# Message passing on one core: the sums move from VectorE's adds to ScalarE's copy and a store into two tables, and the column copies go from 40 to 52 per step

## The chip, the cores and the metric

The kernel runs on one core of a Trainium2 chip. The metric is the device time of one execution in microseconds. The engines that matter are TensorE (PE), VectorE (DVE), ScalarE (ACT), GpSimd (POOL), which issues the gathers, and SyncE (SP), which issues most other DMAs. Each engine has a queue of instructions of its own, which it works through in order.

## The reference

One layer of message passing over a graph of 12500 nodes and 212500 edges, then a residual and a layer norm. `src` and `dst` are the two ends of each edge; the edges come sorted by `dst`.

```python
msg_in = concat([x[src], x[dst], edge_attr])            # 64 + 64 + 32 columns
messages = relu(msg_in @ mW1 + mb1) @ mW2 + mb2         # 128 hidden columns, 64 out
aggregated = segment_sum(messages, dst, 12500)
upd = relu(concat([x, aggregated]) @ uW1 + ub1) @ uW2 + ub2
out = layernorm(x + upd)
```

All is float32. Since the second product is linear, the kernel sums the hidden rows (128 columns) per node and multiplies the sums by the combined weights `wc` = mW2 x uW1; the bias `mb2` comes in by the count of edges of each node.

## The kernel before, in words

**Groups and steps.** The edges are cut into G = 554 groups of 384 (three tiles of 128). The nodes that one group's edges end at lie in a window of W = 32 consecutive nodes. The main loop has a step per group `k`; the order on each engine is the order in which the code is written. Four things are in work at once:

- POOL gathers the source rows `x[src]` of group `k + 16`, one indirect DMA per tile (`gather`, L184), into a ring of 20 buffers `own_s`. A gather may start when the buffer's last user, 20 groups before, is done.
- PE transposes group `k` (`turn`, L429), multiplies group `k - 2` by the message weights (`hidden`, L453), and sums group `k - 4` (`sums`, L481 and L486). The three make one step with a wait in front and a signal behind it; there are two sets of PSUM buffers.
- ACT copies the transposed rows out of PSUM into `own_st` (L440), whose other 32 rows are edge features that SP loads every four steps (L359). SP also loads the window of projected destination rows, `by_dst`, into the moving weights `own_wm`, four steps ahead (L402).
- DVE applies the relu of `hidden` (L464, PSUM to `own_h`), adds the sums of `k - 4` into `own_agg` (L493) and its counts into row 96 of `own_xc` (L494), both at an address held in a register, and writes the one-hot rows of group `k + 6` (`onehot`, L412). The registers of four groups' addresses are loaded by a TENSOR_LOAD (`places`, L371) every fourth step.

**Copied columns.** 54 of the groups aren't gathered. Their 64-row columns are copied one by one from `own_xc`, which holds all of x transposed, into `own_st`: 40 columns per step, at addresses that come from an index tile by TENSOR_LOAD (`registers`, L576; `fetch`, L597 on DVE and L599 on ACT). DVE has `VCOLS = (12, 8)` and ACT `ACOLS = (8, 4, 4, 4)`: one load per entry, then that many copies of 64 x 4 bytes. The copies run from step 18 to step 536. SP fetches the indices of 8 steps at once (L555), and DVE turns them into addresses (L561).

**Update.** When a chunk of 512 nodes has all its sums, six stages turn it into output, one stage per step (`update`): inner (PE, L504 and L505), relu (ACT, L510), outer (PE), stats (DVE), root (ACT), scaled (DVE, then the store of the output). There are 25 chunks, and one is in work at a time. The last ten steps of the loop copy no columns and split the PE step into pieces; the sums of the last groups and the last chunk follow.

A second path, `unordered`, is there for edges whose windows don't fit; it doesn't run on this data.

Of the kernel before, what the change touches and what calls it, by code (L numbers as in the profile page):

```python
# [20 lines left out]
P = 128  # L21
N = 12500
# [15 lines left out]
NW = 2 * SB  # L38
COUNT = 96
NH = 3  # L40
# [9 lines left out]
TIMES = 4  # L50
BEGIN = 18
CHECKED = 8
VCOLS = (12, 8)
ACOLS = (8, 4, 4, 4)
# [49 lines left out]
class Own:  # L104
# [4 lines left out]
    def __init__(self, nc, ctx):  # L109
        def on(name, *shape, of=nc.sbuf_tensor):  # L110
            return ctx.enter_context(of(name, list(shape), F32)).ap()

        self.s = [on(f"own_s{i}", P, TG, D + W) for i in range(RING)]
        self.st = [on(f"own_st{i}", P, SB * GE) for i in range(BLOCKS)]
# [8 lines left out]
        self.agg = on("own_agg", P, NP)  # L123

        self.ps = [[on(f"own_ps{i}{k}", P, 512, of=nc.psum_tensor) for k in range(3)]
                   for i in range(2)]
# [3 lines left out]
def ordered(ctx: ExitStack, tc: tile.TileContext, a, own, ok):  # L130
# [14 lines left out]
    xc, agg = own.xc, own.agg  # L145
    xc_bytes = xc.bitcast(U8)

# [74 lines left out]
    def rest(n0, n1):  # L222

        nc.scalar.activation(xc[D : COUNT + 1, n0:n1],
                             ident[D : COUNT + 1, D : D + 1].to_broadcast([W + 1, n1 - n0]),
                             AF.Copy)
# [23 lines left out]
    def zeroed(k):  # L250

        n0, n1 = (NP * i // BITS for i in (k, k + 1))
        nc.vector.memset(agg[:, n0:n1], 0.0)

    halves = [(0, G // 2), (G // 2, G)]
    firsts_f = [own.ps[k][2][:, : g1 - g0] for k, (g0, g1) in enumerate(halves)]
# [22 lines left out]
    start_i = const.tile([1, G], I32, name="start_i")  # L279
    start_b = const.tile([1, G], I32, name="start_b")  # L280

    def placed():

        for f, (g0, g1) in zip(firsts_f, halves):
            nc.vector.tensor_scalar(start_f[:, g0:g1], f[0:1, :], 0.0, None, ALU.max)
        nc.vector.tensor_tensor(start_f, start_f, high, ALU.min)
        nc.vector.tensor_copy(start_i, start_f)
        nc.vector.tensor_scalar(start_b, start_f, 4.0 * H, None, ALU.mult)
# [4 lines left out]
    ux = const.tile([COUNT + 1, H], F32, name="ux")  # L293
# [3 lines left out]
    def update_weights():  # L297

        nc.vector.memset(ux, 0.0)
# [11 lines left out]
    starts, rows_at, indices, columns_by = {}, {}, {}, {}  # L311
# [4 lines left out]
    by_dst = dram.tile([NP, H], F32, name="by_dst")  # L316
    written = []

    up = None

    def combined():

        wps = ups.tile([H, CH], F32, name="u_ps").rearrange("p (n h) -> p n h", n=4)
        nc.tensor.matmul(wps[:, 0], w2t, u1s, start=True, stop=True)
        nc.tensor.matmul(wps[0:1, 1], b2, u1s, start=True, stop=True)
        nc.vector.tensor_copy(wc, wps[:, 0])
        nc.vector.tensor_copy(ux[COUNT : COUNT + 1, :], wps[0:1, 1])

    def ordered_edges():
# [10 lines left out]
        wrong = temp.tile([1, 2, G], F32, name="wrong")  # L340
# [4 lines left out]
        nc.vector.tensor_tensor(wrong[:, 1], first_f, high, ALU.is_gt)  # L345
        nc.vector.tensor_reduce(nwrong, wrong, mybir.AxisListType.XY, ALU.add)
# [8 lines left out]
    def inputs(b):  # L355
# [3 lines left out]
        efs_by[b] = nc.sync.dma_start(own.st[b % BLOCKS][D + W :, : c1 - c0], a["efT"][:, c0:c1])  # L359
        after(efs_by[b], *([hidden_by[(b - BLOCKS + 1) * SB - 1]] if b >= BLOCKS else []))  # L360

    def columns(g):
        t, c = own.st[g // SB % BLOCKS], (g % SB) * GE
        return t, c, sum(tiles_of(g))

    def places(b):

        g, n = b * SB, min(SB, G - b * SB)
        if n <= 0:
            return  # L370
        _, v = nc.values_load_multi_w_load_instructions(  # L371
            start_i[0:1, g : g + n], engines=[ET.DVE], min_val=0, max_val=N - 1,
            skip_runtime_bounds_check_because="they were clamped to the nodes on the chip",
        )
        for i in range(n):
            starts[g + i] = v[i]
# [13 lines left out]
    def window(g):  # L390
# [3 lines left out]
        if g % SB == 0:  # L394
            n = min(SB, G - g)
            _, v = nc.values_load_multi_w_load_instructions(
                start_b[0:1, g : g + n], engines=[ET.SP], min_val=0, max_val=4 * H * (N - 1),
                skip_runtime_bounds_check_because="they were clamped to the nodes on the chip",
            )
            rows_at.update(zip(range(g, g + n), v))  # L400
# [21 lines left out]

    def turn(g, ps):
# [3 lines left out]
        xt = ps[0][: D + W, :GE]  # L427
# [7 lines left out]
        def copy(step):  # L435
            t, c, n = columns(g)
            turn_by[g] = step
            r = slice(D if g in columned else 0, D + W)
            copies = [ordered_by_steps(
                after(nc.scalar.activation(t[r, c : c + n], xt[r, :n], AF.Copy), step))]  # L440
# [7 lines left out]
    def hidden(g, ps):  # L448
        t, c, n = columns(g)
        sizes = tiles_of(g)  # L450
        pre = ps[1][:, : TG * H].rearrange("p (j h) -> p j h", h=H)
# [5 lines left out]
        needs = [*copy_by[g], *columns_by.get(g, {}).values(), wm_by[g], efs_by[g // SB],  # L457
                 *(wm_loads[g] if g < NW else ())]

        def relu(step):  # L460
# [7 lines left out]
            for i in relu_by[g]:  # L468
                after(i, step, *([sums_by[g - NH]] if g >= NH else []))
            return relu_by[g]  # L470
# [3 lines left out]
    def sums(g, ps):  # L474
        h, s = own.h[g % NH], own.s[g % RING]
        sizes = tiles_of(g)
        sg = ps[2][:, : TIMES * W].rearrange("p (t w) -> p t w", w=W)
        counted = ps[2][0:1, TIMES * W :][:, :W]
        did = []
        for j, p in enumerate(sizes):  # L480
            did.append(nc.tensor.matmul(  # L481
                sg, h[:p, j, :],
                s[:p, j, D:].unsqueeze(1).to_broadcast([p, TIMES, W]),
                start=j == 0, stop=j == len(sizes) - 1))
        for j, p in enumerate(sizes):
            did.append(nc.tensor.matmul(counted, own.one[:p], s[:p, j, D:],  # L486
                                        start=j == 0, stop=j == len(sizes) - 1))

        def add(step):
            sums_by[g] = step  # L490
            at = bass.ds(starts.pop(g), W)
            count = xc[COUNT : COUNT + 1, at]
            a = after(nc.vector.tensor_tensor(agg[:, at], sg[:, 0, :], agg[:, at], ALU.add), step)  # L493
            return [a, after(nc.vector.tensor_tensor(count, counted, count, ALU.add), step)]  # L494

        return did, [*relu_by[g], *copy_by[g]], add

    def update(base, p, n):
# [3 lines left out]
        def inner():  # L502
            u_ps = ups.tile([H, CH], F32, name="u_ps")
            nc.tensor.matmul(u_ps[:, :q], wc, agg[:, rows], start=True, stop=False)  # L504
            nc.tensor.matmul(u_ps[:, :q], ux, xc[: COUNT + 1, rows], start=False, stop=True)  # L505
# [42 lines left out]
        return [inner, relu, outer, stats, root, scaled]  # L548
# [14 lines left out]
    def registers(k, *parts):  # L563
# [5 lines left out]
        for part in parts:  # L569
# [11 lines left out]
            held[part] = engine, c0, v  # L581

    def fetch(part, first=None):
# [79 lines left out]
    def step_update(g):  # L663

        nonlocal now
        if not now and waiting and waiting[0][0] <= g:
# [6 lines left out]
    users = {part: [[], []] for part in (turn, hidden, sums)}  # L673

    def step(*work):
# [3 lines left out]
        for part, g in work:  # L679
            ps, old = own.ps[g % 2], users[part][g % 2]  # L680
# [7 lines left out]
        for g in [g for part, g, *_ in parts if part is sums]:  # L688
            step_update(g)
        for part, g, _, _, follow in parts:  # L690
            users[part][g % 2] = follow(did[-1])
# [4 lines left out]
    places(0)  # L696
    weights(SB)
    inputs(0)
    for i in (0, 1):
        zeroed(i)  # L700
# [15 lines left out]
    for k in range(G):  # L716
        if k < BITS:
            bit(k)
            if k + 2 < BITS:
                zeroed(k + 2)  # L720
        if 1 < k < len(TABLE):
            projected(k)
        if k == CHECKED:
# [6 lines left out]
            up = ctx.enter_context(tc.tile_pool(name="upd", bufs=2))  # L730
        if k % SB == 2:
            inputs(k // SB + 2)
        if k % SB == 1:
            places(k // SB + 1)
        if k < G - SHORT:
            step((turn, k), *([(hidden, k - 2)] if k > 1 else []),
                 *([(sums, k - 4)] if k > 3 else []))
            made, summed = max(0, k - 1), max(0, k - 3)
# [15 lines left out]
        window(k + SB)  # L754
        for n in range(len(STREAMS)):
# [17 lines left out]
    while summed < G:  # L773
        step((sums, summed))
        summed += 1
    while now or waiting:
        step_update(G)
# [17 lines left out]
def unordered(ctx: ExitStack, tc: tile.TileContext, a, own):  # L795
# [9 lines left out]
    src_sb, dst_sb = (own.agg[:, i * (NF + 1) : (i + 1) * (NF + 1)].bitcast(I32) for i in (0, 1))  # L805
    nc.sync.dma_start(src_sb, src)
    nc.scalar.dma_start(dst_sb, dst[:, : NF + 1])
# [41 lines left out]
    dst_f, away = (own.agg[:, i * (NF + 1) : (i + 1) * (NF + 1)] for i in (2, 3))  # L849
    nc.vector.tensor_copy(dst_f, dst_sb)  # L850
    nc.vector.tensor_scalar(away, dst_f, -1.0, spare, ALU.mult, ALU.add)
# [36 lines left out]
    with tc.tile_pool(name="zef", bufs=3) as efp, tc.tile_pool(  # L888
# [16 lines left out]
        def gather(g):  # L905
            m, p = tiles(g)
            at = 4 * (NF + 1) + g % (NEAR + 2) * 2 * R * H
            s, d = (own.agg[:, at + i * R * H :][:, : R * H].rearrange("p (r h) -> p r h", h=H)
                    for i in (0, 1))
            for j in range(m):  # L910
                t = g * R + j
                for o, table, idx in ((s, by_src, src_sb), (d, by_dst, dst_sb)):
                    nc.gpsimd.indirect_dma_start(
                        out=o[:p, j, :], out_offset=None, in_=table[:, :],
                        in_offset=bass.IndirectOffsetOnAxis(ap=idx[:p, t : t + 1], axis=0),
                    )
            gathered[g] = s, d
# [138 lines left out]
def gnn_layer(ctx: ExitStack, nc, a):  # L1056
# [4 lines left out]
    with tc.manual_schedule():  # L1061
        ordered(tc, a, own, ok)
    good = nc.values_load(ok[0:1, 0:1], min_val=0, max_val=1,
                          skip_runtime_bounds_check_because="a comparison's result")
    with tc.If(good == 0):
        with tc.manual_schedule():
            unordered(tc, a, own)
# [38 lines left out]
```

## Time and profile before

| | |
|---|---|
| median of 3 executions | 1895.83 us (1894.88 to 1898.73) |
| profiled execution | 1894.96 us, of which 1893.1 us is the span of the trace |
| granted TensorE clock, mean | 0.963 |
| gathers (L184) | 1499, 1417.3 us busy |
| DVE: column copies (L597) / relu (L464) / one-hot (L412) | 894.5 / 303.1 / 135.7 us busy |
| DVE: adds of counts (L494) and of sums (L493) | 102.0 / 97.9 us busy |
| ACT: column copies (L599) / copy of turned rows (L440) | 1089.2 / 267.3 us busy |

The busy time of a line is what its instructions took on the engine. Where the rows name DVEq, ACTq or SPq, they mean the engine's queue: a TENSOR_LOAD fills registers there, FUSED_REGOPS computes an address, and neither counts as busy time of the engine, though nothing behind it is issued in that time. "a/b/c" in a row are the shortest, the median and the longest of its instructions in ns.

### The profile page before, as it was taken

The page shows a single profiled execution, that of the slowest core. Times are in us where ns is not written, and L with a number is a line of the kernel's source. Part 1 is how long each engine was busy: PE and PEld are TensorE (multiplying, and loading weights), DVE is VectorE, ACT ScalarE, POOL GpSimd, SP SyncE. Part 2 cuts the span into 40 slices and gives each one's busy share as a digit, 9 for nine tenths or more (in the row PEclk, how much of TensorE's full clock was granted, in tenths as well). Part 3 has the DMA queues.
Part 4 walks back from the last instruction along what each step waited for, and adds up shares of the span by engine and source line. Part 5 has one row for each costly group of instructions (what it writes and reads, how often), then busy time and mean ns, then how long its engine had stood idle before and what let it go on. Part 6 is the DMA issues. An engine that isn't in the chain of part 4 may idle for free. (4 is left out here: it accounts for less than half of the span.)

```text
span 1893.1 us, 60001 instructions
## 1 busy us (share of the span) xinstructions
PE 1336.2 (71%) x12323; PEld 1182.5 (62%) x12323; DVE 1475.6 (78%) x13054; ACT 1385.6 (73%) x11008; POOL 1418.0 (75%) x1506
## 2 busy tenths in 40 slices
PE   5877777757667666777677766776766757666767
PEld 4766666656556555666566665666666656656666
DVE  4468898878878788778887887878878888788763
ACT  3368888877777777777787777777777877777741
POOL 7777777777777777777777777777777777777774
PEclk9789999999999999989998999999999999999998
DMA  5542222222222222222222222222222222222221
GB/s 144 138 98 64 54 51 53 48 51 48 45 53 53 46 52 48 50 49 50 49 53 46 52 45 53 53 46 53 48 51 48 48 51 53 45 54 48 50 48 28
DMA packets 113382, 104.90 MB, mean 55 GB/s; under 512 B 51873, under 2 KB 83246, under 8 KB 113006
## 3 DMA queue, kind: packets, MB, share of 16 engines
q0 software_dynamic: 47968, 49.19, 13.6%
q1 hardware_dynamic: 64194, 51.30, 10.0%
q14 instruction: 272, 2.23, 0.4%
q8 instruction: 104, 1.70, 0.4%
q10 hardware_dynamic: 844, 0.48, 0.1%
HBM read 91.19 MB, written 9.62 MB: 53 GB/s over the span
## 5 line engine op out<-in xcount | busy, mean ns | idle before, releaser
L184 POOL DMA_INDIRECT own_s<-in_x,src_sb x1499 | 1417.3, 945 | 457.9 <-DMA own_s<-in_x,src_sb 206.3
L599 ACT ACTIVATE own_st<-own_xc 64x4 uint8 x10360 | 1089.2, 191 | 66.7 <-issue 18.6
L597 DVE COPY own_st<-own_xc 64x4 uint8 x10376 | 894.5, 191 | 171.1 <-issue 146.9
L429 PE MATMUL own_ps<-own_ident,own_s 128*96 128x128 f32 x1661 | 292.4, 287 | 512.0 <-ACT own_st L599 230.9
L440 ACT ACTIVATE own_st<-own_ps 96x384 f32<-96x384 f32 (+1 forms) x554 | 267.3, 483 | 383.0 <-PE own_ps L486 341.6
L429 PEld LDWEIGHTS own_ps<-own_ident,own_s 128*96 128x96 f32 x1661 | 166.4, 130 | 572.8 <-ACT own_st L599 311.4
L481 PE MATMUL own_ps<-own_s,own_h 128*128 128x128 f32 x3322 | 483.7, 284 | 1.9 <-DVE own_h L464 1.3
L453 PE MATMUL own_ps<-own_wm,own_st 128*128 128x128 f32 x3322 | 479.9, 283 | 0.0
L481 PEld LDWEIGHTS own_ps<-own_s,own_h 128*128 128x128 f32 x3322 | 436.0, 200 | 3.8 <-DVE own_h L464 2.4
L464 DVE TENSOR_SCALAR own_h<-own_ps 128x384 f32<-128x384 f32 x553 | 303.1, 548 | 167.4 <-PE own_ps L486 152.3
L453 PEld LDWEIGHTS own_ps<-own_wm,own_st 128*128 128x128 f32 x3322 | 431.7, 198 | 1.4 <-issue 0.5
L486 PE MATMUL own_ps<-own_s,own_one 128*1 128x32 f32 x3322 | 190.0, 194 | 0.0
L486 PEld LDWEIGHTS own_ps<-own_s,own_one 128*1 128x1 f32 x3322 | 114.5, 84 | 70.1 <-issue 7.2
L412 DVE TENSOR_TENSOR own_s<-iota,dlc 128x96 f32<-128x96 f32 x554 | 135.7, 246 | 0.8
L494 DVE TENSOR_TENSOR own_xc<-own_ps,own_xc 1x32 f32 x554 | 102.0, 184 | 28.8 <-PE u_ps L505 11.0
L493 DVE TENSOR_TENSOR own_agg<-own_ps,own_agg 128x32 f32 x554 | 97.9, 177 | 18.1 <-PE own_ps L486 10.3
L383 PE MATMUL u_ps<-w1b,own_xc 65*128 65x128 f32 x196 | 33.9, 325 | 28.6 <-DMA own_xc<-in_xT 12.6
L383 PEld LDWEIGHTS u_ps<-w1b,own_xc 65*128 65x128 f32 x196 | 28.7, 225 | 31.3 <-issue 20.3
L517 PE MATMUL u_ps<-same,own_xc 65*128 65x64 f32 (+1 forms) x196 | 39.5, 284 | 0.5 <-ACT u L510 0.5
L386 ACT ACTIVATE t<-u_ps 128x512 f32<-128x512 f32 (+1 forms) x25 | 14.7, 587 | 33.4 <-DMA by_dst<-t 16.7
L519 PE MATMUL u_ps<-u,u 128*128 128x64 f32 (+1 forms) x196 | 38.3, 277 | 0.0
L517 PEld LDWEIGHTS u_ps<-same,own_xc 65*128 65x128 f32 (+1 forms) x196 | 29.9, 192 | 2.4 <-ACT u L510 0.8
(60 smaller groups left out, 262.1 us busy)
## 6 DMA issues: line engine op xcount, KB each, us to landing
own_st<-in_efT SPq DMA_DIRECT2D x138, 192.0 KB
own_s<-in_x,src_sb POOLq DMA_INDIRECT x1499
own_wm<-by_dst SPq DMA_DIRECT2D x554, 16.0 KB
by_dst<-t SPq DMA_DIRECT2D x24, 256.0 KB
out<-o SPq DMA_DIRECT2D x24, 128.0 KB
own_xc<-in_xT SPq DMA_DIRECT2D x12, 179.2 KB
index<-in_src_copied SPq DMA_DIRECT2D x64, 1.2 KB
dlc_i<-in_dst_cols SPq DMA_DIRECT2D x1, 807.0 KB
```

What stands on the lines that cost most here:

```text
L184: nc.gpsimd.indirect_dma_start(out=s[:p, j, :D], out_offset=None, in_=x[:, :], in_offset=bass.IndirectOffsetOnAxis(ap=src_sb[:p, g * TG + ...
L412: places_by[g] = nc.vector.tensor_tensor(own.s[g % RING][:, :, D:], iota.unsqueeze(1).to_broadcast([P, TG, W]), dlc[:, g * TG : (g + 1) * ...
L429: nc.tensor.transpose(xt[:, j * P : j * P + p], sides[g] if g in sides and j == TG - 1 else s[:p, j, :], ident[:p, :p])
L440: after(nc.scalar.activation(t[r, c : c + n], xt[r, :n], AF.Copy), step))]
L453: nc.tensor.matmul(pre[:p, j, :], t[:, c + j * P : c + j * P + p], wm[g % NW], start=True, stop=True)
L464: relu_by[g] = [nc.vector.tensor_scalar(h, pre, 0.0, None, ALU.max)]
L481: did.append(nc.tensor.matmul(sg, h[:p, j, :], s[:p, j, D:].unsqueeze(1).to_broadcast([p, TIMES, W]), start=j == 0, stop=j == len(sizes) - 1))
L486: did.append(nc.tensor.matmul(counted, own.one[:p], s[:p, j, D:], start=j == 0, stop=j == len(sizes) - 1))
L493: a = after(nc.vector.tensor_tensor(agg[:, at], sg[:, 0, :], agg[:, at], ALU.add), step)
L494: return [a, after(nc.vector.tensor_tensor(count, counted, count, ALU.add), step)]
L597: by[engine] = nc.vector.tensor_copy(o, x_at)
L599: by[engine] = nc.scalar.activation(o, x_at, AF.Copy)
```

## The change

**Sums and counts.** PE's `sums` now has the one-hot rows (32 columns) on the stationary side and the hidden rows on the moving side, so that a group's sums are 32 rows of 128, with the count as column 129. They go into rows 64 to 95 of the PSUM buffer that holds the transposed rows of the same step, beside them. ACT's copy of the turned rows takes 513 columns instead of 384 and moves both. SP then stores 64 rows of 129 floats (the 32 nodes of the window, and 32 rows of zeros behind them) into a table in DRAM, at the address of the group's first node; even and odd groups go to two tables, `by_node0` and `by_node1`. DVE's adds, their address computations, `own_agg` and the loads of `places` are gone; SP's register loads hold two addresses per group. `hidden` is 3 steps behind `turn` instead of 2, and `sums` 6 instead of 4; the PSUM buffer of `hidden` is one of its own, `own_pre`.

**Update.** A chunk starts two steps later and has twelve stages: a load of its rows from both tables (two DMAs), one step of waiting, the transposed counts (PE), their copy (ACT), the transposed sums, added over both tables in PSUM (PE), their copy (DVE, 128 x 512), and then the six stages of before, with three products in `inner`.

**Columns.** `VCOLS = (12, 8, 8)` and `ACOLS = (8, 8, 8)`: 52 columns per step instead of 40, 28 on DVE (20 before) and 24 on ACT (20 before), three loads on each. 71 groups are copied instead of 54, so there are 1448 gathers instead of 1499, and the copies run to step 542. A copy is written as 64 x 1 float instead of 64 x 4 bytes.

```diff
-VCOLS = (12, 8)
-ACOLS = (8, 4, 4, 4)
+VCOLS = (12, 8, 8)
+ACOLS = (8, 8, 8)
+SLOTS = 2
+TO_HIDDEN, TO_SUMS = 3, 6
+ROW = H + 1
+STORED = 2 * W
+SETTLED = 2
+tables = [dram.tile([NP + STORED, ROW], F32, name=f"by_node{i}") for i in range(2)]
...
+    def store(g):
+        t, c, _ = columns(g + TO_SUMS)
+        table = tables[g % 2].rearrange("n w -> (n w)").bitcast(U8)
+        store_by[g] = nc.sync.dma_start(
+            table[bass.ds(store_at.pop(g), 4 * STORED * ROW)].rearrange("(n b) -> n b", n=STORED),
+            t[D:, c + GE : c + GE + ROW].bitcast(U8))
...
     def turn(g, ps):
...
+            if step in with_sums:
+                n = GE + ROW
             copies = [ordered_by_steps(
-                after(nc.scalar.activation(t[r, c : c + n], xt[r, :n], AF.Copy), step))]
+                after(nc.scalar.activation(t[r, c : c + n], ps[r, :n], AF.Copy), step))]
...
     def sums(g, ps):
...
-        def add(step):
-            at = bass.ds(starts.pop(g), W)
-            count = xc[COUNT : COUNT + 1, at]
-            a = after(nc.vector.tensor_tensor(agg[:, at], sg[:, 0, :], agg[:, at], ALU.add), step)
-            return [a, after(nc.vector.tensor_tensor(count, counted, count, ALU.add), step)]
+        for out_ps, of in ((counted, lambda j, p: own.one[:p]), (found, lambda j, p: h[:p, j, :])):
+            for j, p in enumerate(sizes):
+                did.append(nc.tensor.matmul(out_ps, s[:p, j, D:], of(j, p), start=j == 0,
+                                            stop=j == len(sizes) - 1))
...
-        return [inner, relu, outer, stats, root, scaled]
+        return [found, settled, counts, count_moved, all_sums, moved, inner, relu, outer, stats, root, scaled]
...
     def fetch(part, first=None):
...
-            o = t.bitcast(U8)[:D, 4 * (first_c + c) : 4 * (first_c + c + 1)]
-            x_at = xc_bytes[:D, bass.ds(at - own.at, 4)]
+            o = t[:D, first_c + c : first_c + c + 1]
+            x_at = xc_bytes[:D, bass.ds(at - own.at, 4)].bitcast(F32)
```

DVE's queue in the middle of the run, one step of before, from relu to the last column copy (`own_xc` is x transposed, `own_st` the operands of `hidden`, ISA an address computation, 49 the semaphores' suffix):

```order
L464 TENSOR_SCALAR own_h<-own_ps 128x384 [waits PE_49]
L493 ISA
L493 TENSOR_TENSOR own_agg<-own_ps,own_agg 128x32 [waits DVE_49]
L494 ISA
L494 TENSOR_TENSOR own_xc<-own_ps,own_xc 1x32 [waits DVE_49]
L576 TENSOR_LOAD index
L597 COPY own_st<-own_xc 64x4 x12
L412 TENSOR_TENSOR own_s<-iota,dlc 128x3x32
L576 TENSOR_LOAD index
L597 COPY own_st<-own_xc 64x4 x8
```

The same step of DVE after the change (`own_operands` takes the place of `own_st`, `own_rows` that of `own_s`):

```order
L493 TENSOR_SCALAR own_h<-own_pre 128x384 [waits PE_49]
L645 TENSOR_LOAD index
L666 COPY own_operands<-own_xc 64x1 x12
L430 TENSOR_TENSOR own_rows<-iota,dlc 128x3x32
L645 TENSOR_LOAD index
L666 COPY own_operands<-own_xc 64x1 x8
L645 TENSOR_LOAD index
L666 COPY own_operands<-own_xc 64x1 x8
```

The four rows of the adds are gone, and a third load with eight copies stands at the end of the step.

ACT's queue before, one step from the copy of the turned rows on:

```order
L440 ACTIVATE own_st<-own_ps 96x384 [waits PE_49]
L576 TENSOR_LOAD index
L599 ACTIVATE own_st<-own_xc 64x4 x8
L576 TENSOR_LOAD index
L599 ACTIVATE own_st<-own_xc 64x4 x4
```

ACT's queue after, from the same copy on (in this step the group is a copied one, so that 32 rows are moved and not 96):

```order
L469 ACTIVATE own_operands<-own_ps 32x513 [waits PE_49]
L645 TENSOR_LOAD index
L668 ACTIVATE own_operands<-own_xc 64x1 x8
L645 TENSOR_LOAD index
L668 ACTIVATE own_operands<-own_xc 64x1 x8
L645 TENSOR_LOAD index
L668 ACTIVATE own_operands<-own_xc 64x1 x8
```

Before, two more loads of four columns each follow the rows shown; after, three loads of eight are all.

SP's queue after, with the new stores between the window loads (by_node_177 and by_node_178 are the two tables):

```order
L420 DMA own_wm<-by_dst 32x512 [waits DMAHW4_49,PE_49]
L445 DMA by_node_177<-own_operands 64x516 [waits DMAHW0_49,Activation_49]
L420 DMA own_wm<-by_dst 32x512 [waits DMAHW6_49,PE_49]
L445 DMA by_node_178<-own_operands 64x516 [waits DMAHW7_49,DMAHW3_49,Activation_49]
```

Before, the window loads stand next to each other there, with nothing that waits for ACT.

More of the change, by code (lines that the diff above doesn't have):

```diff
@@ L469, in relu @@
                 after(i, step, *([sums_by[g - NH]] if g >= NH else []))
+                tc.declare_no_dep(i.ins, group="relu", keep=before.get("relu", []),
+                                  reason="TensorE's step has read what the last turn of the ring wrote")
+                tc.add_to_no_dep_group("relu", i.ins)
+                before["relu"] = [i.ins]
             return relu_by[g]
@@ L1066, in gnn_layer @@
         with tc.manual_schedule():
[L1067 removed]
+            unordered(tc, a, own, last)
 def kernel(**inputs):
```

233 lines of the change are left out of this document (146 added, 87 removed).

## The prediction

> **What bounds the kernel now.** The page comes first (span, busy shares, the costliest groups). The profiled execution took 1894.96 us for a span of 1893.1, 0.9 under the median of 1895.83; the sum below is made against this span.
>
> ```profile
> span 1893.1 us, 60001 instructions
> PE 1336.2 (71%) x12323; PEld 1182.5 (62%) x12323; DVE 1475.6 (78%) x13054; ACT 1385.6 (73%) x11008; POOL 1418.0 (75%) x1506
> L184 POOL DMA_INDIRECT own_s<-in_x,src_sb x1499 | 1417.3, 945 | 457.9 <-DMA own_s<-in_x,src_sb 206.3
> ```
>
> No engine is full, and DVE has the most busy time. Yet 945 ns of gather and 457.9/1499 = 0.305 us of idle time give 1.25 us per gather, and 1499 of them give 1875 us, nearly the whole span. Whether that pace is POOL's own is told by its gathers in stretches of time, first without column copies (5 to 60 us), then with them:
>
> ```profile
> 5.00:60.00 55.00, 41.89 (x44) 0.89 0.56 144
> 300.00:600.00 300.00, 226.84 (x241) 0.98 0.22 49
> 1500.00:1800.00 300.00, 226.79 (x241) 0.99 0.22 50
> L184 POOL DMA_INDIRECT own_s<-in_x,src_sb x6: 894/944/946, 1869.7 to 1875.9; - x6
> ```
>
> 55/44 = 1.25 and 300/241 = 1.245: the same pace everywhere. So POOL bounds this kernel, and the last gather starts at 1875.9. A step needs 3 gathers, less those that the 40 copied columns save: 3 x (1 - 40/384) x 1.25 = 3.36 us.
>
> What would bound it next shows early, where POOL is ahead. Gathers issued (POOL) and tiles transposed (PE) up to 147 and 232 us, relus (L464, DVE) up to 147, and then the relus of a stretch:
>
> ```profile
> 0.00:147.00 147.00, 109.30 (x115) 0.88 0.50 127
> 0.00:232.00 232.00, 173.57 (x183) 0.93 0.41 100
> ...
> 0.00:147.00 147.00, 18.73 (x96) 12.44 (x96) 0.88 0.50 127
> 0.00:232.00 232.00, 32.90 (x180) 20.53 (x180) 0.93 0.41 100
> ...
> 0.00:147.00 147.00, 15.51 (x28) 0.88 0.50 127
> L464 DVE TENSOR_SCALAR own_h<-own_ps x40: 524/542/559, 166.8 to 279.0; 128x384 f32<-128x384 f32 x40
> ```
>
> 115 gathers against 96 tiles at 147 us; 183 against 180 at 232, of which 12 belong to copied groups and need none. PE could run ahead and doesn't: one relu (L464) follows another after 112.2/39 = 2.88 us. That is VectorE's own step, and inside one step it looks so (DVE, then its queue and ScalarE's in one stretch):
>
> ```profile
> 920.23 0.54 DVE L464 TENSOR_SCALAR own_h<-own_ps 128x384 f32<-128x384 f32 x1
> ...
> 921.19 1.00 DVE L597 COPY own_st<-own_xc 64x4 uint8 x12
> 922.10 0.24 DVE L412 TENSOR_TENSOR own_s<-iota,dlc 128x96 f32<-128x96 f32 x1
> 922.27 0.65 DVE L597 COPY own_st<-own_xc 64x4 uint8 x8
> 922.84 0.55 DVE L464 TENSOR_SCALAR own_h<-own_ps 128x384 f32<-128x384 f32 x1
> L576 DVEq TENSOR_LOAD <-index x13: 593/843/849, 917.6 to 934.5; - x13
> L493 DVEq FUSED_REGOPS  x7: 76/76/76, 917.3 to 934.2; - x7
> L494 DVEq FUSED_REGOPS  x7: 93/93/93, 917.5 to 934.4; - x7
> L371 DVEq TENSOR_LOAD <-start_i x139: 339/344/681, 10.5 to 1864.8; - x139
> ```
>
> The quickest step is 922.84 - 920.23 = 2.61 us, back to back. In it DVE's queue loads 12 registers (0.849), then 8 (0.593 to 0.597), and computes two addresses (0.076 and 0.093); 2.61 - 0.849 - 0.597 - 0.169 = 1.00 us is left for 24 issues (20 copies, one-hot, relu, two adds), 0.041 each. While it loads it issues nothing, and the pieces add up to the step: the bound of DVE is its queue, not its 2.4 us of work. From 2.61 to 2.88 comes what isn't in every step: L371 every fourth, an update's statistics, the index multiplication, pauses in issue.
>
> **The change, part by part, on DVE's queue.** (a) Removed: two adds, their two address computations, L371. In the stretch above the load starts 0.3 us after the first address computation (917.6 against 917.3): 0.169 for the two, the rest for the adds, 2 x 0.041 = 0.08 and a little waiting. I take -0.32 (bounds -0.25 and -0.35), and -0.10 for L371 (0.344 and two issues, over four steps). (b) Added: a third load of 8 registers, +0.597, by the row of the same form; and 8 copies, +0.32 at 0.04 each (bounds: 0, if they were issued for nothing, and 0.65, the engine's time for the 8 in the rows above). The copies change from four bytes to one float, and no row shows that form; I take its issue as unchanged, since the queue sets it and a copy remains one instruction. (c) A move of 128 x 512 per update, one issue in about 22 steps, and more instructions per step, so more pauses: +0.01.
>
> Step after: 2.88 - 0.32 - 0.10 + 0.60 + 0.32 + 0.01 = 3.39 us. POOL's step becomes 3 x (1 - 52/384) x 1.25 = 3.24. So DVE's queue is past POOL by 0.15 us per step, and **the bound moves from POOL to DVE's queue**.
>
> The other engines, in the same stretch:
>
> ```profile
> L576 ACTq TENSOR_LOAD <-index x25: 306/310/553, 917.3 to 934.2; - x25
> 920.57 2.08 ACT L599 ACTIVATE own_st<-own_xc 64x4 uint8 x20
> L440 ACT ACTIVATE own_st<-own_ps x7: 467/486/486, 917.3 to 934.2; 96x384 f32<-96x384 f32 x6, 32x384 f32<-32x384 f32 x1
> L510 ACT ACTIVATE u<-u_ps x25: 347/574/599, 144.4 to 1883.9; 128x512 f32<-128x512 f32 x24, 128x212 f32<-128x212 f32 x1
> L402 SPq DMA_DIRECT2D own_wm<-by_dst x31: 315/316/1895, 906.5 to 997.9; - x31
> ```
>
> ACT: its loads go from 0.553 + 3 x 0.310 = 1.48 to 3 x 0.553 = 1.66 us, four copies more cost 4 x 2.08/20 = 0.42 on the engine, and the copy of 513 columns takes 0.58 (L510) instead of 0.486. 24 x 0.104 + 0.58 = 3.08 on the engine at most, under DVE's 3.39; its queue, 1.66 and 25 issues at 0.046, 2.8. Hidden, with 0.3 us to spare. SP: a store per step, 0.32 us to issue as L402 has, beside one window load; 0.7 of 3.4 us, hidden in the loop. In the start, where windows wait on the projected rows, 18 stores cost 18 x 0.32 = 6 us, against the 5 us that hidden gains by being a step later. The store waits for its step's copy, and the next window load stands behind it; that load is 4 steps early, so hidden. PE: the moving side of the sums is the same count of columns; hidden under 3.39.
>
> End of the run:
>
> ```profile
> 1848.00:1877.00 29.00, 26.40 (x233) 21.97 (x233) 12.99 (x49) 4.56 (x10) 21.78 (x24) 1.00 0.15 31
> 1882.54 0.19 DVE L493 TENSOR_TENSOR own_agg<-own_ps,own_agg 128x32 f32 x1 [1.29 <-PE own_ps L486]
> 1887.97 0.52 ACTq L546 DMA_DIRECT2D out<-o  x1
> ```
>
> PE (26.40 of 29) is full in the last ten steps, which before hold 10 turns, 12 hiddens and 14 sums and now one hidden and two sums more: about 33 us. From the last add to the end before: 10.6 us. Now the last sums are copied (0.58), stored, read back, transposed twice by PE and copied (about 2.5 in all), before the same 10.6; the two transfers are bounded by 1 us and by the 4.6 from the end of the last out issue (1888.5) to the span's end; I take 2.5 each. The chunk before it, two steps and six stages later, is in front: about 7 us. Together 26 (bounds 18 and 33).
>
> Sum: step 30 by 145 us (28 relus by 147 before, and relu is two steps behind); 513 steps x 3.39 = 1739; +33 +26 = 1943; +1.9 around the span = 1945, and 0.9 for the median: **1946 us**. Each 0.1 us of step is 51 us.
>
> **Rivals.** *POOL stays the bound (faster).* If one copy's issue costs 0.02 less in the new form, 28 of them take 0.56 off and DVE's step is 2.83; it decides at 3.24, that is 0.15 less than my sum, 0.005 per copy or half of (b)'s 0.32. Then 1448 gathers end at 3 + 1448 x 1.25 = 1813; 7 us from the last gather to the last sums as before (1875.9 to 1882.5), 3 more for the backlog, and 26: 1849 + 2 = 1851. For it: nothing here measures the issue of the one-float form, and the 0.041 is a remainder. Against: the three loads, in which nothing is issued, are 2.04 us alone, and 30 issues then have to fit into 1.2.
> By the Trainium skill ("Runtime: NRT & Kernel Launch", section "Instruction fetch mechanics") the sequencer issues one instruction in about 20 cycles; at the 0.96 GHz that "VectorE: DVE Perf Modes" (section "Specifications") gives, an estimate of 0.02 us, so by it this rival would hold. The row's 0.041 disagrees, and the row decides.
>
> *DVE's copies block POOL (much slower).* If 28 float copies of 0.07 each held POOL up, a step would be up to 3.24 + 2.0 = 5.2 us and the time 2800; half of it, 2300. Against: the 20 copies of the four-byte form, which fill half of each step, leave the gather at 1.245 us against 1.25 without them.
> [...]
>
> *A draw.* At a step of 3.29 the time is that of before (145 + 513 x 3.29 + 59 + 2 = 1894), the third load half hidden.
>
> **How the numbers follow.** DVE's queue bounds, step 3.32 to 3.45: 0.62 (1910 to 1980). POOL blocked: 0.04. Draw, within 0.2% (about what a measurement of this kernel can tell from no change): 0.06. POOL bounds: 0.28. Slower by over 0.2%: 0.66. The range takes in the faster case's foot and the upper bounds of the step: 1848 to 1980.
>
> **What would show it.** Right: 849 + 597 + 597 ns of DVE loads per step; relus 3.39 us apart on average and 3.2 at the quickest; POOL's idle time per gather above 0.305, and released by the ring, while PE finds its gathers landed. Wrong: gathers still 1.25 us apart to the end (the first rival), a gather well over 945 ns (the second), or ACT's step, 3.08 at most, ending the wait of PE; then ACT's 24 copies or the copy of 513 columns were mis-sized. The tail is right if the last sums lie 18 to 33 us before the end.

## The result, and the profile after

The changed kernel takes 2002.9 us (median of 4 executions, 1998.7 to 2003.88) against 1895.36 us of the kernel before: 1.0561 times as long, 95% interval 1.054 to 1.0583. The forecast was slower, at 1946 us with a range up to 1980; the direction was right, and the loss of 107 us is twice the 51 that were forecast. The profiled execution took 1998.7 us for a span of 1996.4. In most of the runs below every execution, of the kernel before too, took 2525 us or more, with pauses in issue on several engines whose cause was not found; such a time, called a long one, stands beside that of the kernel before and is compared with it alone.

The page of the changed kernel, first its span and busy shares, then the gathers and the column copies on ScalarE and VectorE:

```profile
span 1996.4 us, 67325 instructions
PE 1475.0 (74%) x13157; PEld 1198.2 (60%) x13157; DVE 1491.0 (75%) x16278; ACT 1648.3 (83%) x13265; POOL 1369.5 (69%) x1455
L193 POOL DMA_INDIRECT own_rows<-in_x,src_sb x1448 | 1368.7, 945 | 526.6 <-issue 235.1
L668 ACT ACTIVATE own_operands<-own_xc 64x1 f32 x12576 | 1298.8, 189 | 63.3 <-DVE own_h L493 28.1
L666 DVE COPY own_operands<-own_xc 64x1 f32 x14688 | 1029.9, 136 | 358.8 <-issue 300.2
```

51 gathers are gone, but the idle time before them went from 457.9 to 526.6 us: 0.364 us per gather instead of 0.305. GpSimd now waits. VectorE's copies (L666) idle for 300.2 us on "issue", that is, on their own queue. The gathers of the changed kernel in two stretches of 300 us:

```profile
300.00:600.00 300.00, 224.68 (x238) 0.97 0.31 65
1500.00:1800.00 300.00, 210.99 (x225) 0.95 0.31 63
```

Before, there were 241 in each. Now there are 238, and 225 late in the run. What a gather waits for is a copy on ScalarE, which the kernel takes as the mark that its ring buffer is free; nobody waits for a gather but the next gather. From the answer on line L193 for the whole run:

```profile
L193 POOL DMA_INDIRECT own_rows<-in_x,src_sb x1448: 898/944/1327, 2.9 to 1896.0; - x181
...
  ACT own_operands L469: 132.5, 169
  ACT own_operands L668: 119.0, 380
...
who waited for it (us, times):
  POOL own_rows L193: 32.9, 108
```

VectorE's step, in the same stretch of the run as before, its queue's loads there, and its relus in the loop with what they waited for:

```profile
920.65 0.54 DVE L493 TENSOR_SCALAR own_h<-own_pre 128x384 f32<-128x384 f32 x1
921.36 0.81 DVE L666 COPY own_operands<-own_xc 64x1 f32 x12 [0.17 <-issue]
922.10 0.24 DVE L430 TENSOR_TENSOR own_rows<-iota,dlc 128x96 f32<-128x96 f32 x1
922.44 0.57 DVE L666 COPY own_operands<-own_xc 64x1 f32 x8
923.36 0.57 DVE L666 COPY own_operands<-own_xc 64x1 f32 x8 [0.35 <-issue]
923.85 0.54 DVE L493 TENSOR_SCALAR own_h<-own_pre 128x384 f32<-128x384 f32 x1
L645 DVEq TENSOR_LOAD <-index x17: 591/597/854, 917.2 to 934.9; - x17
L493 DVE TENSOR_SCALAR own_h<-own_pre x514: 523/539/559, 151.6 to 1928.8; 128x384 f32<-128x384 f32 x172
  PE own_ps L514: 18.4, 11
```

An undisturbed step is 923.85 - 920.65 = 3.20 us, back to back, with the engine idle for 0.17 and 0.35 us behind the first and the third load (a step behind a longer one can be shorter, down to 2.7 us). The relus of the last rows run from step 30 to step 543: 513 steps in 1777.2 us, 3.464 each. Only 11 of them made the engine wait for TensorE, for 18.4 us in all; else its own queue alone held it up. The end of the run, from the copy of the last sums on:

```profile
1962.38 0.27 ACT L524 ACTIVATE own_operands<-own_ps 32x129 f32<-32x129 f32 x1 [3.87 <-PE own_ps L514]
...
1971.33 0.40 SPq L615 DMA_DIRECT2D out<-o  x1
1971.84 1.11 SPq L536 DMA_DIRECT2D found<-by_node  x2
...
1977.04 0.51 PE L546 MATMUL u_ps<-own_ident,found 106*1 106x106 f32 x2 [8.90 <-SPq L1155]
1979.66 1.22 PE L546 MATMUL u_ps<-own_ident,found 106*1 106x106 f32 x6 [2.11 <-SPq L1155]
...
1983.39 0.38 DVE L566 COPY agg<-u_ps 128x212 f32<-128x212 f32 x1 [12.09 <-PE u_ps L546]
1983.82 1.08 PE L572 MATMUL u_ps<-agg,wc 128*128 128x212 f32 x2 [0.47 <-DVE agg L566]
1991.04 0.52 ACTq L615 DMA_DIRECT2D out<-o  x1
```

From the last sums (1962.65) to the end are 33.8 us, against 10.6 from the last add before. Four parts: the chunk in front needs until its output store at 1971.3; the last chunk's two loads, issued from 1971.84 on, are there for TensorE at 1977.04 and 1979.66; counts, sums and their copies take until 1983.8; the update proper takes the last 12.6.

### The profile page after: what moved, and what is told of

The parts are those of the page before. It is cut to its first block, busy times and chain, and to the rows that moved or that the text cites. A ratio compares the mean times of both kernels' runs of the same rounds, so it can differ in the third digit from the quotient of the medians.

```text
span 1996.4 us, 67325 instructions
## 1 busy us (share of the span) xinstructions
PE 1475.0 (74%) x13157; PEld 1198.2 (60%) x13157; DVE 1491.0 (75%) x16278; ACT 1648.3 (83%) x13265; POOL 1369.5 (69%) x1455
## 5 line engine op out<-in xcount | busy, mean ns | idle before, releaser
L193 POOL DMA_INDIRECT own_rows<-in_x,src_sb x1448 | 1368.7, 945 | 526.6 <-issue 235.1
L668 ACT ACTIVATE own_operands<-own_xc 64x1 f32 x12576 | 1298.8, 189 | 63.3 <-DVE own_h L493 28.1
L666 DVE COPY own_operands<-own_xc 64x1 f32 x14688 | 1029.9, 136 | 358.8 <-issue 300.2
L456 PE MATMUL own_ps<-own_ident,own_rows 128*96 128x128 f32 x1661 | 293.2, 288 | 418.9 <-ACT own_operands L469 268.9
L482 PE MATMUL own_pre<-own_wm,own_operands 128*128 128x128 f32 x3322 | 483.0, 284 | 0.7 <-DVE own_h L493 0.7
L514 PE MATMUL own_ps<-own_h,own_rows 128*32 128x128 f32 x3322 | 472.9, 280 | 0.0
L469 ACT ACTIVATE own_operands<-own_ps 96x513 f32<-96x513 f32 (+2 forms) x554 | 323.8, 584 | 159.0 <-PE own_ps L514 138.8
L482 PEld LDWEIGHTS own_pre<-own_wm,own_operands 128*128 128x128 f32 x3322 | 435.9, 200 | 3.2 <-issue 1.8
L493 DVE TENSOR_SCALAR own_h<-own_pre 128x384 f32<-128x384 f32 x553 | 298.8, 540 | 91.0 <-PE own_ps L514 59.3
L514 PEld LDWEIGHTS own_ps<-own_h,own_rows 128*32 128x32 f32 x3322 | 331.5, 114 | 4.4 <-issue 0.2
L400 ACT ACTIVATE t<-u_ps 128x512 f32<-128x512 f32 (+1 forms) x25 | 14.6, 585 | 38.2 <-PE u_ps L397 19.1
L579 ACT ACTIVATE u<-u_ps 128x512 f32<-128x512 f32 (+1 forms) x25 | 14.7, 586 | 38.0 <-PE u_ps L574 38.0
```

The costliest lines, as they stand in the source:

```text
L193: nc.gpsimd.indirect_dma_start(out=s[:p, j, :D], out_offset=None, in_=x[:, :], in_offset=bass.IndirectOffsetOnAxis(ap=src_sb[:p, g * TG + ...
L456: nc.tensor.transpose(xt[:, j * P : j * P + p], sides[g] if g in sides and j == TG - 1 else s[:p, j, :], ident[:p, :p])
L469: after(nc.scalar.activation(t[r, c : c + n], ps[r, :n], AF.Copy), step))]
L482: nc.tensor.matmul(pre[:p, j, :], t[:, c + j * P : c + j * P + p], wm[g % NW], start=True, stop=True)
L493: relu_by[g] = [nc.vector.tensor_scalar(h, pre, 0.0, None, ALU.max)]
L514: did.append(nc.tensor.matmul(out_ps, s[:p, j, D:], of(j, p), start=j == 0, stop=j == len(sizes) - 1))
```

## The experiments

Theory A: VectorE's queue, with its three register loads, sets the step. Rival B: ScalarE sets it (24 copies, three loads, a copy of 513 columns). Rival C: the sums' new path (stores, longer copy) slows every step.

**VectorE back to 20 columns, ScalarE left as changed.**

```diff
 # the changed kernel
-VCOLS = (12, 8, 8)
+VCOLS = (12, 8)
```

> The changed kernel with VectorE at 20 columns in two loads (12, 8) and ScalarE left at 24 in three: 44 columns, about 60 copied groups, so some 1482 gathers. Theory A (VectorE's queue sets the step): its quickest step falls from 3.20 to 2.28 us, GpSimd's gathers become the bound again at 3 x (1 - 44/384) x 1.25 = 3.32 us per step, the last gather starts near 1855 us, and the end comes some 41 us behind it (7 to the last sums as before, 34 from there as in the changed kernel): about 1898 us. Theory B (ScalarE, whose work is unchanged here, sets the step): the step stays at 3.46 us and the time near 2000 us. Theory C (the stores and the longer copy cost the time wherever they stand): near 2000 us too.

And for the two later runs, dve20_2 and dve20_3:

> VectorE 20 columns in two loads, ScalarE 24 in three, again, since the first time fell on a chip on which every engine pauses in its issue for 0.5 to 1.3 us at a time and the kernel before takes 2530 us. Where the kernel before takes its 1895 us: theory A (VectorE's queue sets the changed kernel's step) 1898 us, with GpSimd's gathers 1.25 us apart; theory B (ScalarE sets it) about 2000 us.

> VectorE 20 columns in two loads, ScalarE 24 in three, once more, one look. Where the kernel before takes 1895 us: theory A (VectorE's queue sets the changed kernel's step) 1898 us with gathers 1.25 us apart; theory B (ScalarE) about 2000 us. Where it takes 2530 to 2570 us, 2600 to 2635 as before.

Measured (dve20_3, one execution): 1900.2 us, the kernel before 1895.07 beside it. The gathers of this run:

```profile
300.00:600.00 300.00, 226.84 (x241) 0.96 0.33 70
1500.00:1800.00 300.00, 226.84 (x241) 0.92 0.32 67
L193 POOL DMA_INDIRECT own_rows<-in_x,src_sb x1481: 898/944/1482, 2.9 to 1854.1; - x186
L493 DVE TENSOR_SCALAR own_h<-own_pre x514: 524/557/559, 149.6 to 1823.8; 128x384 f32<-128x384 f32 x172
```

241 gathers per 300 us again, the last at 1854.1 where 1855 was expected, and 1900.2 us where 1898 was expected. ScalarE's 24 copies and three loads, the stores and the one-float form are those of the changed kernel, so B and C fall; eight columns and a load on VectorE are the difference of 100 us. The step is (1823.8 - 149.6)/513 = 3.26 us, at GpSimd's pace.

The long times of the same kernel are 2603.35 us against 2530.4 (dve20; ratio 1.0294, 1.0243 to 1.0344) and 2633.56 against 2568.95 (dve20_2; 1.0254, 1.0234 to 1.0274).

**ScalarE to 16 columns, VectorE left as changed.**

```diff
 # the changed kernel
-ACOLS = (8, 8, 8)
+ACOLS = (8, 8)
```

> The changed kernel with ScalarE at 16 columns in two loads (8, 8) and VectorE left at 28 in three: 44 columns. Theory A (VectorE's queue): the step stays at 3.46 us, the time within 10 us of the changed kernel's 2003. Theory B (ScalarE): ScalarE loses 8 copies and a load, some 0.75 us per step, so GpSimd bounds at 3.32 us per step and the time is about 1898 us. Between the two, about 1970, if both take turns in ending the wait of a step.

And for act16_2 and act16_3:

> VectorE 28 columns in three loads, ScalarE 16 in two, again for the same reason. Where the kernel before takes 1895 us: theory A within 10 us of 2003 us and a step of 3.46 us; theory B about 1898 us; about 1970 if both take turns in ending the wait of a step.

> VectorE 28 columns in three loads, ScalarE 16 in two, once more. Where the kernel before takes 1895 us: theory A (VectorE's queue) within 10 us of 2003 us and relus 3.46 us apart; theory B (ScalarE) about 1898 us; about 1970 if both take turns in ending the wait of a step.

All three times are long ones: 2660.51 us against 2530.4 (act16; 1.0501, 1.0455 to 1.0547), 2693.71 against 2568.95 (act16_2; 1.0483, 1.0431 to 1.0535), 2647.9 against 2535.37 (act16_3). Beside the kernel above, which copies 44 columns too, it is slower by 57 us (act16 and dve20) and by 60 (act16_2 and dve20_2). That points to VectorE, but what it takes where the kernel before takes 1895 us was not measured.

**The changed kernel again**, to tie the long times to it (after_again).

> The changed kernel itself, unmodified, beside the kernel before, to tie the other runs to it: where the kernel before takes 1895 us, 2003 us as before. On a chip on which all engines pause longer in their issue (kernel before 2530 to 2570 us): theory A (VectorE's queue, whose instructions per step went from 27 to 33) 5% over the kernel before, some 2660 to 2690, as with ScalarE's columns taken away (2661 and 2694 there); theory B (ScalarE) clearly above that kernel, 2720 or more.

2659.0 us against 2568.09: 1.035 (1.0312 to 1.0389). A gave 5% for it and 2660 to 2690 us; the ratio missed that, and it also lies below the 4.8 and 5.0% of the kernel with 16 columns on ScalarE, which has less to copy. The change costs 3.5% here and not 5.6%, so the long times cannot size a step of the forecast.

**The sums' new path alone, with the columns of before.**

```diff
 # the changed kernel
-VCOLS = (12, 8, 8)
-ACOLS = (8, 8, 8)
+VCOLS = (12, 8)
+ACOLS = (8, 4, 4, 4)
```

> The changed kernel with the columns of before, (12, 8) and (8, 4, 4, 4): the sums by ScalarE's copy and the stores alone. Theory A: VectorE's step is 2.28 us at the quickest, GpSimd bounds as in the kernel before, 1499 gathers of 1.25 us, the last at 1876 us; the end is 41 us behind it instead of 17: about 1919 us, 1.2% over the kernel before. Theory C (the stores or the copy of 513 columns slow each step): well over that, 1950 or more. If the longer start (6 us in the changed kernel) shifts the gathers too, 1925.

And for sums_alone_2, sums_alone_3 and sums_alone_4:

> The sums by ScalarE's copy and the stores with the columns of before, once more. Where the kernel before takes 1895 us: theory A, 1919 us (gathers bound, 1499 of them, the end 41 us behind the last gather instead of 17); theory C (the stores or the longer copy slow each step) 1950 or more.

> The sums by ScalarE's copy and the stores with the 40 columns of before. Where the kernel before takes 1895 us: theory A, 1919 us: GpSimd's 1499 gathers bound, the last starts at 1876, and the end is 41 us behind it instead of 17; theory C, 1950 or more.

> The sums by ScalarE's copy and the stores with the 40 columns of before. Where the kernel before takes 1895 us: theory A, 1919 us: GpSimd's 1499 gathers bound, the last starts at 1876, and the end is 41 us behind it instead of 17; theory C (the stores or the longer copy slow each step), 1950 or more.

Measured (sums_alone_4): 1923.84 us, the kernel before 1895.61 beside it. Its gathers, and its span from the page:

```profile
L193 POOL DMA_INDIRECT own_rows<-in_x,src_sb x1499: 898/944/1645, 2.9 to 1875.3; - x188
span 1922.1 us, 60880 instructions
```

The last gather starts at 1875.3, as before the change (1875.9): neither the stores nor the longer copy, nor the later start, slow the loop while gathers bound it. The end lies 46.8 us behind the last gather instead of 17.2. So the new path by itself costs 28 us, all of it behind the last gather; 24 were expected. The long times are 2591.18 us against 2530.4 (sums_alone; 1.0234, 1.0184 to 1.0285), 2592.83 against 2535.37 (sums_alone_2) and 2590.62 against 2542.58 (sums_alone_3).

**The 52 columns alone, with VectorE's adds as they were.**

```diff
 # the kernel before
-VCOLS = (12, 8)
-ACOLS = (8, 4, 4, 4)
+VCOLS = (12, 8, 8)
+ACOLS = (8, 8, 8)
```

> The kernel before with the columns of the change, (12, 8, 8) and (8, 8, 8), sums by VectorE's adds as they were. Theory A: VectorE's quickest step is 2.61 + 0.60 (third load) + 0.32 (8 copies) = 3.53 us, with the rest 3.8, so about 147 + 510 x 3.8 + 45 = 2130 us: the columns are the cause, and the change's removal of the adds gives part of it back. Theory C (the sums' new path is the cause): GpSimd bounds with 1448 gathers, the last at 1813, the end at 1832 us.

And for before52_2, before52_3 and before52_4:

> The kernel before with the 52 columns, sums by VectorE's adds, once more. Where the kernel before takes 1895 us: theory A, 2130 us, VectorE's step 3.53 us at the quickest and 3.8 on average; theory C (the sums' new path is the cause), 1832 us.

> The kernel before with the 52 columns of the change, sums by VectorE's adds. Where the kernel before takes 1895 us: theory A (VectorE's queue), 2130 us, with a step of 3.53 us at the quickest and 3.8 on average, so that the columns are the cause and the removal of the adds gives part of it back; theory C (the sums' new path is the cause), 1832 us.

> The kernel before with the 52 columns of the change, sums by VectorE's adds as they were. Theory A (VectorE's queue): 2130 us, with a step of 3.53 us at the quickest and 3.8 on average, so that the columns are the cause and the removal of the adds gives part of it back. Theory C (the sums' new path is the cause): GpSimd bounds with 1448 gathers, 1832 us.

Measured (before52_4): 2173.28 us, the kernel before 1895.37 beside it. One of its steps on VectorE, the relus from step 30 to step 543, and its gathers late in the run:

```profile
1000.49 0.54 DVE L464 TENSOR_SCALAR own_h<-own_ps 128x384 f32<-128x384 f32 x1
1004.01 0.54 DVE L464 TENSOR_SCALAR own_h<-own_ps 128x384 f32<-128x384 f32 x1
L464 DVE TENSOR_SCALAR own_h<-own_ps x514: 524/541/559, 146.8 to 2125.9; 128x384 f32<-128x384 f32 x172
1500.00:1800.00 300.00, 190.38 (x202) 0.92 0.19 42
```

3.52 us for this step (3.53 expected), (2125.9 - 146.8)/513 = 3.86 on average (3.8 expected), and 202 gathers instead of 241. So more columns alone cost 278 us, the sums alone 28, and both together 107: moving the adds away does take 3.86 - 3.464 = 0.39 us per step off VectorE's queue, but only a queue that bounds has use for it, and it bounds because of the third load and its eight copies. The long times of this kernel are 2592.64 us against 2530.4 (before52; 1.0242, 1.0195 to 1.0289), 2595.23 against 2535.37 (before52_2) and 2594.54 against 2542.58 (before52_3): 2% there, 15% here. Why the same columns cost so little there was not worked out.

**The copy of a chunk's sums on ScalarE.**

```diff
 # the changed kernel, stage moved
-            nc.vector.tensor_copy(agg[:, :q], ps[:, :q])
+            nc.scalar.activation(agg[:, :q], ps[:, :q], AF.Copy)
```

> The changed kernel with the copy of a chunk's sums (128 x 512, stage `moved`) on ScalarE instead of VectorE. Where the kernel before takes 1895 us: if the update's stages on VectorE's queue are what the forecast left out, the 19 steps of the loop with that copy fall from 3.97 us to about 3.2 to 3.4 and the time falls by 12 to 17 us, to about 1988; if ScalarE is as near to its limit as VectorE, no change (2003). On a chip where the kernel before takes 2530 us or more, 2630 to 2660.

1981.89 us (one execution), the kernel before 1898.29 beside it: 17 us below the changed kernel's profiled execution and 21 below its median, where 12 to 17 were expected; the four executions of the changed kernel lie within 5 us. The relus of this run from step 30 to step 543 with what they waited for, and then what TensorE waited for from 300 to 1800 us in the changed kernel:

```profile
L493 DVE TENSOR_SCALAR own_h<-own_pre x514: 524/540/558, 153.0 to 1908.4; 128x384 f32<-128x384 f32 x172
  PE own_ps L514: 1.7, 1
PEld u_ps L572 <- DVE agg L566: 31.7, 19, 2.1
```

The loop takes 1755.4 us instead of 1777.2, 21.8 less, about 1 us per chunk; the start and the end give 5 back. In the changed kernel the copy stands in VectorE's queue behind the step's 28 column copies; TensorE, whose next stage needs it, waits 31.7/19 = 1.7 us for it, once per chunk. With the copy on ScalarE this wait is 0.7 us once in the run, and the relus' own wait for TensorE falls from 18.4 us to 1.7.

Not every chunk pays for that wait. Of the 23 copies in the loop, nine are followed by a relu that waits for TensorE, 7 to 11 us behind them, for 14.7 us in all; the other 14 are not, and the two waits that are left stand ahead of the first copy. What sets the nine apart is TensorE's granted clock, which is the number behind the bracket in these rows (10 us from a copy of the 14 and from one of the nine, and the late relu of the latter):

```profile
891.73:901.73 10.00, 9.28 (x67) 1.00 0.28 56
1046.05:1056.05 10.00, 9.28 (x26) 0.53 0.12 27
1056.55 0.56 DVE L493 TENSOR_SCALAR own_h<-own_pre 128x384 f32<-128x384 f32 x1 [3.88 <-PE own_ps L514]
```

Behind each of the nine the clock is 0.53 to 0.83 on average over 10 us, behind each of the 14 it is 1.00, and with the copy on ScalarE it is 1.00 behind all 23. So TensorE's wait and the late relu go together with a fall of the clock; that the wait brings the fall about fits both runs, but no run tests it by itself.

**46 columns in the kernel before**, as a version that might beat both: `VCOLS = (12, 10)`, `ACOLS = (8, 8, 8)`, two loads on VectorE.

> The kernel before with 46 columns, VectorE (12, 10) and ScalarE (8, 8, 8), sums by VectorE's adds: 63 copied groups, about 1473 gathers. Theory A: VectorE's quickest step is 2.61 + 0.13 (two registers more) + 0.08 (two copies) = 2.82 us, on average 3.1, under GpSimd's 3 x (1 - 46/384) x 1.25 = 3.30, so the last gather starts at 1843 and the end is 17 us behind: about 1862 us, 1.8% under the kernel before. Theory B: ScalarE's 24 copies bound at 3.46 us: 1950 or more.

And for before46_2:

> The kernel before with 46 columns, VectorE (12, 10) and ScalarE (8, 8, 8), sums by VectorE's adds. Theory A: VectorE's step is 2.61 + 0.13 (two registers) + 0.08 (two copies) = 2.82 us at the quickest, 3.1 on average, under GpSimd's 3 x (1 - 46/384) x 1.25 = 3.30; some 1473 gathers, the last near 1843, the end 17 us behind: about 1862 us, 1.8% under the kernel before. If ScalarE's 24 copies bound, 1950 or more.

Both times are long ones: 2887.65 us against 2535.37 (before46; 1.1382, 1.1344 to 1.1419) and 2900.55 against 2569.45 (before46_2). Its copies in the first of them, on ScalarE and VectorE, then its register loads, and VectorE's of the changed kernel in a long execution (after_again):

```profile
L599 ACT ACTIVATE own_st<-own_xc 64x4 uint8 x12412 | 1316.2, 191 | 915.3 <-issue 908.5
L597 DVE COPY own_st<-own_xc 64x4 uint8 x11396 | 947.0, 177 | 1119.4 <-issue 1107.1
L576 ACTq TENSOR_LOAD <-index x1552: 314/1733/2250, 175.6 to 2816.3; - x194
L576 DVEq TENSOR_LOAD <-index x1036: 848/1851/3119, 176.0 to 2822.0; - x173
L645 DVEq TENSOR_LOAD <-index x1574: 344/598/1166, 178.9 to 2575.3; - x197
```

Some 1000 us of idle time on "issue" stand here on each engine, against 214 and 338 in the long execution before52, and the register loads explain it. Two kinds of them alternate from step to step: 8 registers take 0.55 or 1.76 us, 12 take 0.85 or 2.74, 10 take 1.08 or 2.29 (medians). Which kind a load is follows from the place of its first entry in the index tile: at a multiple of four entries it is the short one, two entries off it is the long one, in all 2588 loads of the run. With 46 columns per step half of the loads start off a multiple of four; with 40, 44 and 52 none does, and there no median is above 0.85 us. So the expectation failed at "+0.13 (two registers more)". VectorE's loads are (0.85 + 1.08 + 2.74 + 2.29)/2 = 3.48 us per step on average here, and if they take that where the kernel before takes 1895 us, which was not measured, its step is 4.7 us with 26 issues and two address computations, an estimate: far slower than before. No version was found that beats the kernel before.

## Why the prediction was right in direction and wrong in size

Right: the bound moved from GpSimd to VectorE's queue; the loads were 0.85 + 0.60 + 0.60 us; an undisturbed step was 3.20 us, GpSimd's idle time per gather rose above 0.305, and only the next gather waits for a gather. ScalarE, SP and TensorE, with the work of the change, keep a step of 3.26 us (dve20_3), so they do not set the loop, but for the waits for TensorE above.

Wrong: the sum, against the profiled execution's own time (1945 forecast, 1998.7 measured, 53.7 us), term by term:

| term | forecast | measured | difference |
|---|---|---|---|
| step 30 at | 145 | 151.6 | +6.6 |
| 513 steps | 1739 (3.39 each) | 1777.2 (3.464 each) | +38.2 |
| step 543 to the last sums | 33 | 33.9 | +0.9 |
| last sums to the end | 26 | 33.8 | +7.8 |
| around the span | 1.9 | 2.3 | +0.4 |

Two terms of the step's sum failed. The first is its start, 2.88 us. It was read off 39 steps of the kernel before, and these hold the work of one chunk's update on VectorE, where the loop has one in 22 steps. The rows of that stretch and of the changed kernel's loop (four statistics per update), and the relus around the step with the scaling in that stretch:

```profile
L526 DVE BATCH_NORM_STATS2 stats<-u_ps x4: 198/198/219, 220.3 to 221.3; 128x6 f32<-128x64 f32 x4
L595 DVE BATCH_NORM_STATS2 stats<-u_ps x92: 197/199/217, 195.3 to 1921.7; 128x6 f32<-128x64 f32 x92
224.53 0.54 DVE L464 TENSOR_SCALAR own_h<-own_ps 128x384 f32<-128x384 f32 x1
228.63 0.55 DVE L464 TENSOR_SCALAR own_h<-own_ps 128x384 f32<-128x384 f32 x1
```

That step takes 4.10 us, the one with the statistics 3.97, and the other 37 take 2.81 each. In the changed kernel 46 steps with statistics or scaling take 4.56 us, the 23 with the copy of a chunk's sums 4.01, and the other 444 take 3.32, which is what the sum gives for them: 2.81 + 0.51. So the steps without an update came out as worked out. An update's two steps add about 2.5 us, as in the stretch; but 23 of them are 57 us, and the average of the stretch carried 32 into the sum: 25 us are missing.

The second is (c), "+0.01" for the copy of a chunk's sums. It was priced as one issue on VectorE's queue, 5 us over the loop; it cost 21.8 (moved_act), two thirds of it as the relus' wait for TensorE behind nine of the copies, which the sum has nowhere. Together the two terms fall short by 25 + 17 = 42 us; the loop's difference is 38.2, and the 4 us between are not explained.

The other terms: in the kernel before the relu of step 30 starts at 147.0, so 145 was 2 us early before any change. With the old path of the sums and 52 columns it starts at 146.8 (before52_4), with the new path at 149.6 to 153.0 (dve20_3, moved_act), where the sum had 1 us for the path; a store took 0.48 us to issue instead of 0.32, and the rest was not taken apart. In the end of the run the working named the parts, and each was too short: the chunk in front took 8.7 us, not 7; the loads took until 8.3 us behind it, where store and loads had 5; the transposes and copies took 4.2 where 3.1 were taken, and the update proper 12.6, not 10.6. The profiled execution was also the quickest of the four; the median lies 4.2 us above it, not 0.9.

The rivals: that GpSimd stays the bound is excluded, since the issue of a one-float copy is no cheaper: the undisturbed step came out at 3.20, where 2.61 + 0.60 + 0.32 - 0.32 gives 3.21. The three loads leave 3.20 - 2.04 = 1.16 us for 30 issues, 0.039 each. The Trainium skill ("Runtime: NRT & Kernel Launch", section "Instruction fetch mechanics") has some 20 cycles per instruction as the floor of issue, 0.02 us by the estimate in the prediction; the 0.039 lies above that floor, and a step worked out from the floor is too short. That float copies hold GpSimd up is excluded for this form: with 20 of them per step (dve20_3) there are 241 gathers per 300 us, as with none of them in the kernel before. The Trainium skill ("SBUF — State Buffer", the box on the "DVE blocks DMA" trap) says that a float copy inside SBUF locks GpSimd out of writing descriptors; for copies of one element these gathers show nothing of it.

The range ended at 1980 since its upper bound took 3.45 us per step and next to nothing for the start and the end being longer as well; with 3.46 per step, 7 more in the start and 8 more in the end it would have been 2000.

## What to carry to other kernels

Where an engine's instructions take their addresses from registers, sum its queue: each load of registers stops issue for its whole length (0.6 us for 8 registers, 0.85 for 12), whatever the engine's busy share says. An average step is only worth as much as its stretch: count the rare work in it, here one update in 39 steps against one in 22, before it is multiplied by 513. Work taken off an engine pays only where that engine bounds; here the two halves of a change cost 28 and 278 us alone and 107 together. And an instruction that another engine waits for is priced by its place in its queue, not by its own length: a copy of 0.67 us behind 28 others made TensorE wait 1.7 us each time.

## What the runs showed of the hardware that was not expected

A load of registers from a tile takes about three times as long when its first entry does not lie at a multiple of four: 1.76 us instead of 0.55 for 8 registers on ScalarE, 2.74 instead of 0.85 for 12 on VectorE, in both runs of the kernel with 46 columns. Registers beyond a multiple of four cost more as well: 10 registers took 1.08 us, where 8 take 0.60 and 12 take 0.85.

TensorE's granted clock fell to 0.53 to 0.83 over 10 us behind nine of its 23 waits for the copy of a chunk's sums (1.6 us each on average), and behind none of the 23 copies where that wait was gone. Behind each of the nine a relu came late on VectorE, and behind none of the others.
